# A graph network with dense adjacency tables: where the one-hots of the degrees, the marks for the scatters, the returned rows and the last convolution's loads stand

## The chip, the cores and the metric

The kernel runs on one core of a Trainium2 chip. The metric is the device time of one execution in microseconds; three executions before the change gave 3894.49, 3894.97 and 3899.32, and the median is 3894.97. The engines are called as the profile calls them: PE is the matrix engine (TensorE), PEld its loading of weights, DVE the vector engine, ACT the scalar engine, POOL is GpSimd, SP the queue that issues most DMAs.

## The reference

A matrix x of 3125 nodes by 256 features goes through four graph layers and four feed-forward layers in turn. Each takes a layer norm of x and is added to x. There are 50000 edges (src, dst, edge_weight); dst is sorted. Cut to the parts that matter here:

```python
edge_index = jnp.stack([src, dst])
x = x + L0_gnn(layernorm(x), ...)   # HW = H @ W; segment_sum(edge_weight * HW[dst], src) + b
x = x + L0_ffn(layernorm(x), ...)   # half of the nodes: gelu(sel @ w1 + b1) @ w2 + b2, times a score
x = x + L1_gnn(layernorm(x), ...)   # two convolutions; deg = count of edges per dst, norm = rsqrt(deg)
x = x + L1_ffn(layernorm(x), ...)   # 8 experts, top 2
x = x + L2_gnn(layernorm(x), ...)   # four weighted sums over edges, two projections
x = x + L2_ffn(layernorm(x), ...)   # 8 experts, top 2
x = x + L3_gnn(layernorm(x), ...)   # two convolutions with counts, layer norms and silu
x = x + L3_ffn(layernorm(x), ...)   # 8 experts, top 1 with a capacity
```

All of it is float32. The degree of a node (the number of its edges by dst, plus one) is needed from the second graph layer on.

## The kernel before, in words

**Tables.** The sums over edges are done as dense matrix products. The nodes are padded to 25 tiles of 128, and 3200 by 3200 tables in DRAM hold what the edges add up to: tw the weights, tcn the counts; for the first two tiles of rows a table of pairs, tp, holds both. The edges lie in 391 chunks of 128. DVE compares the edges' cells with each other (L547), so that each cell is written once; then one indirect DMA of POOL for each chunk (L595) scatters 128 cells. 118 chunks go into tp, chunks 118 to 390 into tw (273), chunks 106 to 390 into tcn (285). As dst is sorted, a row tile k of a table is complete once the chunks up to a bound are scattered.

**The first product.** `l0_gnn` computes tw times HW in nine parts, cut over the row tiles k at 3, 6, 9, 12, 15, 18, 21, 23 and 25. Each part goes through seven chunks of columns (4 tiles, the last 1). For each chunk it loads a tile tt of the table, and DVE adds the product to x (L903). The first part (`low_part`) reads tp, separates it into weights and counts and writes both to tw and tcn; the eight others read tw. Each load is ordered behind the scatters that its rows need (`gate`).

**Degrees.** `degrees` is a generator. Each step builds, for 16 chunks of edges, two one-hot tiles on DVE (op, 16 by 128, and ot, 16 by 25, L765), and PE sums their products into a 128 by 25 tile of counts (L772). There are 25 such groups; at the end come the largest count, the inverse root and its row broadcast. `product` takes two steps after each chunk, beginning with the first part.

**Marks.** Scatters that no load needs yet are held back. `weights` and `counts` issue groups of chunks, and a group stands "behind" a mark, an instruction given with `self.pace(...)`. There are 18 marks: the last sum of each of the nine parts (1 to 9), the end of each of the seven chunks of the first FFN (10 to 16), and two places in the start of `l1_gnn` (17, 18). PACE_W gives the chunks of tw at which the groups are cut, PACE_C those of tcn, counted from chunk 106. Chunks of tw below the first number stand behind no mark.

**Loads and memory.** PE's operands are loaded by SP in program order. A load waits until the memory that it writes is free, so the place of a tile in its pool decides which old tile it waits for; everything behind it in SP's queue waits too. Three such places matter:

- The first convolution of `l1_gnn` streams tcn (L256), while SP also loads small tiles of later layers, among them a tile "flat" for a bias (L150), which lies on the memory of the counts and their indices, cnt and idx_c.
- After the second FFN (experts, `tiles`), ACT's queue loads the returned rows of both experts of each node into a ring zt, and DVE adds them to x (L2012). Then `L2_gnn` loads a weight W0 (L143), and `spmm_rows` streams tw (L297).
- Before the last graph layer, SP loads its two weights (L143), the affine parameters gamma and beta (L1349), the condition (L1351), and then streams tcn (L256) for `spmm`.

L265 and L305 are the matrix products of these layers, L893 that of the first. The two lines that step the degrees are

```python
                    for _ in range(2):
                        next(degrees, None)
```

and the marks of the parts are given by

```python
            self.pace(last)
            ...
                for a, z in parts[1:]:
                    self.pace(product(stream, a, z, kb, 24 // kb))
```

Of the kernel before, what the change touches and what calls it, by code (L numbers as in the profile page):

```python
# [10 lines left out]
F32 = mybir.dt.float32  # L11
# [8 lines left out]
P = 128  # L20
# [4 lines left out]
D = 256  # L25
# [3 lines left out]
NC = EC + 1  # L29
# [24 lines left out]
PAIRS = last_chunk(LOW * P) + 1  # L54


PACE_W = (235, 260, 286, 311, 337, 363, NC)
PACE_C = (16, 40, 72, 122, 142, 162, 183, 203, 223, 247, 252, 264)


class Net:
# [681 lines left out]
    def degrees(self, pool):  # L743

        nc = self.nc
        dst_i = pool.tile([P, NC], I32, name="dst_i")
        nc.vector.tensor_copy(dst_i, self.col["dst"])

        def part(name, op, by):
            i = pool.tile([P, NC], I32, name=f"{name}_i")  # L750
            nc.vector.tensor_scalar(i, dst_i, by, None, op0=op)
            t = pool.tile([P, NC], F32, name=name)
            nc.vector.tensor_copy(t, i)
            return t

        dp, dt = part("dst_p", ALU.bitwise_and, P - 1), part("dst_t", ALU.logical_shift_right, 7)
        iota = self.psum()
        nc.vector.tensor_copy(iota[:, :P], self.iota)
        deg = self.psum()[:, :NT]
        for g in self.groups:  # L760
            n, a, b = len(g), g[0], g[-1] + 1
            op = pool.tile([P, 2 * GROUP, P], BF16, tag="op", name=self.name("op"), bufs=2)
            ot = pool.tile([P, 2 * GROUP, NT], BF16, tag="ot", name=self.name("ot"), bufs=2)
            for o, d, m in (op, dp, P), (ot, dt, NT):
                nc.vector.tensor_tensor(  # L765
                    o[:, :n, :],
                    d[:, a:b, None].to_broadcast([P, n, m]),
                    iota[:, None, :m].to_broadcast([P, n, m]),
                    op=ALU.is_equal,
                )  # L770
            for i, c in enumerate(g):
                nc.tensor.matmul(deg, lhsT=op[:, i, :], rhs=ot[:, i, :], start=c == 0, stop=c == NC - 1)  # L772
            yield
        most, all_ = pool.tile([P, 1], F32, name="most"), pool.tile([1, P], F32, name="all")
        nc.vector.tensor_reduce(most, deg, AX.X, ALU.max)
        ps = self.psum()
        nc.tensor.transpose(ps[0:1, :P], most, self.ident)
        nc.vector.tensor_copy(all_, ps[0:1, :P])
        few = pool.tile([1, 1], F32, name="few")
        nc.vector.tensor_reduce(few, all_, AX.X, ALU.max)  # L780
        nc.vector.tensor_scalar(self.few_i, few, 4095.5, None, op0=ALU.is_lt)
        root = pool.tile([P, NT], F32, name="root")
        nc.scalar.activation(root, deg, AF.Sqrt, bias=self.ones[:, 0:1])
        nc.vector.reciprocal(self.dinv, root)
        self.broadcast_row(self.dinv, self.dinv_row)
# [60 lines left out]
    def l0_gnn(self, keep, ordered, clear, fill):  # L846


        nc, ins, x = self.nc, self.ins, self.x
        score = keep.tile([P, NT, 1], F32, name="score")  # L850
        wr, br = keep.tile([P, KD, 1], F32, name="wr0"), keep.tile([1, 1], F32, name="br0")
        nc.sync.dma_start(wr, ins["L0_ffn_wr"].rearrange("(k p) o -> p k o", p=P))
        nc.sync.dma_start(br, ins["L0_ffn_br"].rearrange("(o n) -> o n", o=1))
        with self.reusing("l0g") as pool:
            hw = self.hw
            fm0 = self.nm_tile("fm0").rearrange("p t d -> p (t d)").rearrange("p (k n) -> p k n", k=KD)
            degrees = self.degrees(pool)
            half = len(clear) // 2
            for part in clear[:half]:
                part()  # L860

            def chunk(t0, nt):
                s = slice(t0 * P, (t0 + nt) * P)
                nn = self.normed(pool, t0, nt)
                nc.vector.tensor_add(x[:, t0 : t0 + nt, :], x[:, t0 : t0 + nt, :], nn[:, :nt, :])
                yield
                yield
                yield
                self.to_fm(nn, 0, nt, lambda k, ps: self.copy(k, fm0[:, k, s], ps))
                yield from self.logits_fm(pool, fm0[:, :, s], t0, nt, wr, br, score)  # L870


            rows = self.tw[0:V, :].rearrange("(k p c) o -> p k (c o)", p=P, c=NP)
            steps = iter(())
            kend = KEND[ordered]
            parts = list(zip((0,) + kend, kend))

            def product(stream, a, z, kb, bufs):
                nonlocal steps
                for t0, nt in CHUNKS:  # L880
                    tt = stream.tile([P, kb, 512], F32, tag="tt", name=self.name("tt"), bufs=bufs)
                    tt = tt[:, : z - a, : nt * P]
                    if a or not ordered:
                        ld = nc.sync.dma_start(tt, rows[:, a:z, t0 * P : (t0 + nt) * P])
                        self.gate(ordered, ld, "w", z * P)
                    else:
                        self.low_part(stream, tt, t0, nt)
                    for i0 in range(0, nt, 2):
                        m = min(2, nt - i0)
                        ps = self.psum()[:, : m * D]  # L890
                        for i in range(m):
                            for j in range(a, z):
                                nc.tensor.matmul(  # L893
                                    ps[:, i * D : (i + 1) * D],
                                    lhsT=tt[:, j - a, (i0 + i) * P : (i0 + i + 1) * P],
                                    rhs=hw[:, j, :],
                                    start=j == a,
                                    stop=j == z - 1,
                                )
                                if (j - a) % 3 == 2 or j == z - 1:  # L900
                                    next(steps, None)
                        part = x[:, t0 + i0 : t0 + i0 + m, :].rearrange("p t d -> p (t d)")
                        last = nc.vector.tensor_add(part, part, ps)  # L903
                    for _ in steps:
                        pass
                    for _ in range(2):
                        next(degrees, None)
                    if z == NT:
                        steps = chunk(t0, nt)
                        next(steps)  # L910
                return last

            with self.reusing("low") as stream:
                last = product(stream, *parts[0], parts[0][1], 2)
            for part in clear[half:]:
                part()
            fill()
            self.pace(last)
            with self.reusing("high") as stream:
                kb = max(z - a for a, z in parts)  # L920
                for a, z in parts[1:]:
                    self.pace(product(stream, a, z, kb, 24 // kb))
                for _ in steps:
                    pass
        return fm0, score[:, :, 0]

# [410 lines left out]
    def l3_gnn(self, after, ordered):  # L1337
        nc, ins = self.nc, self.ins
        g = lambda s: ins[f"L3_gnn_{s}"]
        if not ordered:  # L1340
            self.few = self.truth(self.few_i)
        with self.reusing("l3g", side="right") as pool:
            ws = [self.square(pool, f"L3_gnn_W{l}") for l in (1, 2)]
            wide = lambda s: pool.tile([P, D], F32, name=self.name(s))
            aff, cond = [], []
            for l in (1, 2):
                aff.append([wide(s) for s in ("gamma", "beta")])
# [29 lines left out]
            h = pair("h")  # L1377
            bounds = [0, 1, 2, 5, 10, 15, 20, 25]
            for t0, t1 in zip(bounds, bounds[1:]):
# [11 lines left out]
                for i in range(n):  # L1391
                    a = pool.tile([P, 1, D], F32, tag="aff", name=self.name("aff"), bufs=3)
# [6 lines left out]
            h2 = pair("h2")  # L1399
# [23 lines left out]
                yield from after(pool, t0, nt)  # L1423

            def body(dt):
                self.spmm(self.tcn, h, pool, first, dt, 3, lead=2)
                self.spmm(self.tcn, h2, pool, second, dt, 3)

            if ordered:
                body(F32R)  # L1430
# [212 lines left out]
class Experts:  # L1643
# [253 lines left out]
    def tiles(self, pool, side, then):  # L1897
        net, nc, ins, tc = self.net, self.nc, self.ins, self.net.tc
        name, ht, affine, func, summed = self.name, self.ht, self.affine, self.func, self.summed
        rows, z, pars = self.rows, self.z, self.pars  # L1900
        ring = lambda s, shape, n: [pool.tile(shape, F32, name=net.name(s)) for _ in range(n)]
        xbs, pars_, b2s = ring("xb", [P, D + 2], 4), ring("par", [P, self.np_], 4), ring("b2", [P, D], WBUFS)
        ybs, zts = ring("yb", [P, D], 4), [] if summed else ring("zt", [P, 2, 4, D], 4)
        w1s, w2s = zip(*((*ring("w1", [P, KD, ht * P], 1), *ring("w2", [P, ht, D], 1)) for _ in range(WBUFS)))
        why = "counts of experts, at most 7, and truths"

# [174 lines left out]
```

## Time and profile before

| what | us |
|---|---|
| median of three executions | 3894.97 |
| the profiled execution | 3892.81 |
| its span | 3890.8 |
| PE busy | 3484.7 |
| DVE busy | 1324.0 |
| POOL busy | 1060.2 |
| ACT busy | 789.6 |
| one-hots on DVE, op / ot (L765, 25 each) | 55.8 / 13.9 |
| matmuls of the degrees on PE (L772, 391) | 13.9 |
| scatters into tw (L595, 273) | 267.7 |
| scatters into tcn (L595, 285) | 285.6 |

The profiled execution is 2.2 us below the median, and its span, from the first to the last instruction, is 2.0 us below its own time. Times "at" a number of us below are counted from the start of that span. A wait's releaser is what ended it; where several things were waited for, it is the last by the profile.

The stages on that scale: tables to about 350, the first product to 688, the first FFN to 906, the second graph layer from 938 on, returned rows of the second FFN from 1598, the third graph layer from 1642, the fourth from 3234, the last FFN from about 3600.

### The profile page before, as it was taken

What the parts mean: (1) busy time and instruction counts of PE and PEld (TensorE: products, weight loads), DVE (VectorE), ACT (ScalarE), POOL (GpSimd) and SP (SyncE); (2) the same over time, 40 slices, a digit from 0 to 9 for tenths busy, and PEclk for the clock granted to TensorE, in tenths of its full rate; (3) what the DMA queues carried; (4) which work ended last, traced back from release to release, by engine and by line L of the source; (5) the groups of instructions that cost most, each with busy time, mean ns of one, the idle gap of its engine ahead of it and who ended that gap; (6) DMA issues with size and microseconds to landing.
All of it is one profiled execution on the core that took longest, in us unless ns stands there. A gap on an engine that the chain in (4) does not pass through costs nothing. (4 is left out here: it accounts for less than half of the span.)

```text
span 3890.8 us, 45871 instructions
## 1 busy us (share of the span) xinstructions
PE 3484.7 (90%) x16848; PEld 2638.2 (68%) x16848; DVE 1324.0 (34%) x4523; ACT 789.6 (20%) x1748; POOL 1060.2 (27%) x1020
## 2 busy tenths in 40 slices
PE   6775979899799789599999999999899997999698
PEld 4654867557687579488744688644599996877344
DVE  9976214944014553400000000022441116323333
ACT  3320000213012234200000000011244445222222
POOL 5776557777200045100000000000133330000232
PEclk7767989989899899799999999999999998999799
DMA  8789334002677389644444444444344557686441
GB/s 325 285 281 328 102 102 125 1 1 82 213 232 230 121 283 347 200 155 158 152 136 148 139 149 152 150 155 157 120 106 109 171 145 248 219 265 217 101 99 30
DMA packets 430038, 655.67 MB, mean 169 GB/s; under 512 B 62929, under 2 KB 206057, under 8 KB 429804
## 3 DMA queue, kind: packets, MB, share of 16 engines
q1 hardware_dynamic: 366590, 585.97, 45.0%
q0 software_dynamic: 48560, 50.07, 5.8%
q10 hardware_dynamic: 14654, 16.60, 1.3%
q8 instruction: 135, 2.21, 0.2%
q14 instruction: 99, 0.81, 0.1%
HBM read 622.05 MB, written 128.56 MB: 193 GB/s over the span
## 5 line engine op out<-in xcount | busy, mean ns | idle before, releaser
L265 PE MATMUL ps<-tt,h 128*128 128x512 f32 (+1 forms) x2800 | 1074.7, 466 | 52.1 <-DMA tt<-tcn 52.1
L265 PEld LDWEIGHTS ps<-tt,h 128*128 128x128 f32 x2800 | 515.7, 190 | 392.6 <-issue 288.4
L893 PE MATMUL ps<-hw,tt 128*128 128x256 f32 x1250 | 289.1, 392 | 55.2 <-DMA tt<-tw 47.4
L1956 PE MATMUL ps<-xe,w 128*128 128x128 f32 x2688 | 321.5, 276 | 10.5 <-DMA w<-in_L_ffn_W 8.6
L1956 PEld LDWEIGHTS ps<-xe,w 128*128 128x128 f32 x2688 | 317.2, 192 | 18.8 <-issue 11.7
L305 PE MATMUL ps<-n,tt 128*128 128x256 f32 x1250 | 272.2, 381 | 46.4 <-DMA tt<-tw 46.4
L1965 PE MATMUL ps<-w,hid 128*128 128x256 f32 x1344 | 312.7, 383 | 0.0
L595 POOL DMA_INDIRECT tw<-tot,idx_w x273 | 267.7, 980 | 156.3 <-issue 80.4
L595 POOL DMA_INDIRECT tcn<-cnt,idx_c x285 | 285.6, 1002 | 89.7 <-issue 86.2
L893 PEld LDWEIGHTS ps<-hw,tt 128*128 128x128 f32 x1250 | 244.1, 198 | 92.0 <-issue 47.5
L305 PEld LDWEIGHTS ps<-n,tt 128*128 128x128 f32 x1250 | 239.0, 191 | 79.7 <-issue 46.8
L1237 POOL DMA_DIRECT2D L_ffn_z<-x x5 | 3.8, 766 | 1005.6 <-DVE bn L1176 929.6
L305 PE MATMUL ps<-h,tt 128*128 128x256 f32 x1250 | 270.0, 379 | 0.0
L1965 PEld LDWEIGHTS ps<-w,hid 128*128 128x128 f32 x1344 | 248.8, 192 | 29.9
L265 PE MATMUL ps<-tt,lo 128*128 128x512 f32 (+1 forms) x700 | 260.7, 379 | 0.0
L265 PE MATMUL ps<-tt,h_lo 128*128 128x512 f32 (+1 forms) x700 | 259.9, 378 | 0.0
L1959 ACT ACTIVATE hid<-ps,par 128x128 f32<-128x128 f32 x672 | 225.9, 364 | 166.5 <-PE ps L1956 138.6
L305 PEld LDWEIGHTS ps<-h,tt 128*128 128x128 f32 x1250 | 237.5, 190 | 32.3
L1973 POOL DMA_INDIRECT L_ffn_z<-yb,to x112 | 149.1, 1331 | 318.9 <-ACT hid L1959 236.3
L345 PE MATMUL ps<-w,fmc 128*128 128x256 f32 x700 | 173.0, 400 | 17.4 <-ACT fmc L1077 13.8
L1130 DVE TENSOR_SCALAR h<-ps 128x256 f32<-128x256 f32 x24 | 10.2, 425 | 515.8 <-PE ps L305 515.8
L547 DVE SCALAR_TENSOR_TENSOR eq<-cells,dinv_row,ahead 128x256 bf16<-128x256 f32 (+3 forms) x391 | 179.8, 518 | 0.0
(408 smaller groups left out, 3952.1 us busy)
## 6 DMA issues: line engine op xcount, KB each, us to landing
tt<-tw SPq DMA_DIRECT2D x120, 1280.0 KB
tt<-tcn SPq DMA_DIRECT2D x119, 1280.0 KB
w<-in_L_ffn_W SPq DMA_DIRECT2D x112, 1024.0 KB
w<-in_L_ffn_W SPq DMA_DIRECT2D x112, 512.0 KB
tw<-zero_row SPq DMA_DIRECT2D x23, 1600.0 KB
tcn<-zero_row SPq DMA_DIRECT2D x25, 1472.0 KB
tt<-tw SPq DMA_DIRECT2D x36, 768.0 KB
w<-in_L_ffn_w SPq DMA_DIRECT2D x18, 1024.0 KB
```

Source lines behind the costliest of these rows:

```text
L265: nc.tensor.matmul(pair[m], lhsT=part[:, k, m * P : (m + 1) * P], rhs=tt[:, j, :].bitcast(dt), start=k == 0 and i == 0, stop=k == NT - 1 a ...
L305: nc.tensor.matmul(ps[i], lhsT=tt[:, j, i * P : (i + 1) * P], rhs=h[:, k, :], start=k == 0, stop=k == NT - 1)
L345: self.nc.tensor.matmul(ps, lhsT=fm[:, k, i * P : (i + 1) * P], rhs=w[:, k, :], start=k == 0, stop=row is None and k == KD - 1)
L547: nc.vector.scalar_tensor_tensor(eqs[j], cells[k][:, at : at + m], self.col["w"][:, j : j + 1], ahead[:, GROUP * P - m :], op0=ALU.is_equa ...
L595: st = nc.gpsimd.indirect_dma_start(out=table[:, :], out_offset=bass.IndirectOffsetOnAxis(ap=idx[:, c : c + 1], axis=0), in_=src[:, c, :], ...
L893: nc.tensor.matmul(ps[:, i * D : (i + 1) * D], lhsT=tt[:, j - a, (i0 + i) * P : (i0 + i + 1) * P], rhs=hw[:, j, :], start=j == a, stop=j = ...
L1130: nc.vector.tensor_scalar(new[:, t, :], ps, 0.5, None, op0=ALU.mult)
L1237: put(dst[t0 * P : (t0 + full) * P, :].rearrange("(t p) d -> p t d", p=P), src[:, :full, :])
L1956: nc.tensor.matmul(ps, lhsT=w1[:, k, h * P : (h + 1) * P], rhs=xe[:, k, :], start=k == 0, stop=k == KD - 1)
L1959: nc.scalar.activation(hid[:, h, :], ps, func, bias=par[:, h : h + 1])
L1965: nc.tensor.matmul(ps, lhsT=hid[:, h, :], rhs=w2[:, h, :], start=h == 0, stop=h == ht - 1)
L1973: st = nc.gpsimd.indirect_dma_start(out=z[:, :], out_offset=bass.IndirectOffsetOnAxis(ap=self.to[ph][:, 0, j : j + 1], axis=0), in_=yb, in ...
```

## The change

Four edits.

1. `product` takes one step of `degrees` after each chunk instead of two, and none in the first part; those left after the last part are taken then. The one-hots are placed in DVE's order behind the last sum of the chunk (`self.added`), as an order for the scheduler without a semaphore.
2. PACE_W has six numbers instead of seven and begins with 263 instead of 235; PACE_C has thirteen instead of twelve, with other cuts. The 18 marks stay. Behind mark 1 came chunks 235 to 259 of tw, now 263 to 288. The last of tw and the first counts came behind mark 6, now behind mark 5. Behind mark 11 came counts 142 to 161, now 113 to 132; behind mark 18 came counts 264 to 284, now 245 to 284.
3. In `tiles` the ring zt is allocated ahead of xb, par and b2 instead of behind yb.
4. In `l3_gnn` the two weights, gamma, beta, the condition and the streamed tables of both convolutions come from a pool "l3w" on the right side of the memory; the rest stays in "l3g", now on the left side.

```diff
-PACE_W = (235, 260, 286, 311, 337, 363, NC)
-PACE_C = (16, 40, 72, 122, 142, 162, 183, 203, 223, 247, 252, 264)
+PACE_W = (263, 289, 315, 341, 367, NC)
+PACE_C = (2, 28, 45, 62, 93, 113, 133, 153, 173, 194, 205, 229, 245)
...
+        self.added = None
         for g in self.groups:
...
-                nc.vector.tensor_tensor(
+                one = nc.vector.tensor_tensor(
                     o[:, :n, :],
                     d[:, a:b, None].to_broadcast([P, n, m]),
                     iota[:, None, :m].to_broadcast([P, n, m]),
                     op=ALU.is_equal,
                 )
+                if self.added is not None:
+                    self.order(one, self.added, "the products' sums are needed first", sync=False)
...
-                    for _ in range(2):
+                    self.added = last
+                    if a or not ordered:
                         next(degrees, None)
...
-                for _ in steps:
+                for _ in chain(steps, degrees):
                     pass
...
-        with self.reusing("l3g", side="right") as pool:
-            ws = [self.square(pool, f"L3_gnn_W{l}") for l in (1, 2)]
-            wide = lambda s: pool.tile([P, D], F32, name=self.name(s))
+        with self.reusing("l3w", side="right") as held, self.reusing("l3g") as pool:
+            ws = [self.square(held, f"L3_gnn_W{l}") for l in (1, 2)]
+            wide = lambda s: held.tile([P, D], F32, name=self.name(s))
...
-                self.spmm(self.tcn, h, pool, first, dt, 3, lead=2)
-                self.spmm(self.tcn, h2, pool, second, dt, 3)
+                self.spmm(self.tcn, h, held, first, dt, 3, lead=2)
+                self.spmm(self.tcn, h2, held, second, dt, 3)
...
+        zts = [] if summed else ring("zt", [P, 2, 4, D], 4)
         xbs, pars_, b2s = ring("xb", [P, D + 2], 4), ring("par", [P, self.np_], 4), ring("b2", [P, D], WBUFS)
-        ybs, zts = ring("yb", [P, D], 4), [] if summed else ring("zt", [P, 2, 4, D], 4)
+        ybs = ring("yb", [P, D], 4)
```

As the engines' orders are built: in the changed kernel PE, ACT, DVE and POOL issue their instructions in the order of before except in the first product, and in SP's queue the first part's loads of raw pairs stand ahead of the clears of tcn, and the flat load of L150 two loads of tcn later.

## The prediction

> **What bounds the kernel now.** The page's group table comes first, since the chain of waits holds nothing here (four rows at the very end). TensorE (PE) is busy for 90% of the span, and each column "idle before" names what it waits for:
>
> ```profile
> PE 3484.7 (90%) x16848; PEld 2638.2 (68%) x16848; DVE 1324.0 (34%) x4523; ACT 789.6 (20%) x1748; POOL 1060.2 (27%) x1020
> ...
> L265 PE MATMUL ps<-tt,h 128*128 128x512 f32 (+1 forms) x2800 | 1074.7, 466 | 52.1 <-DMA tt<-tcn 52.1
> ...
> L893 PE MATMUL ps<-hw,tt 128*128 128x256 f32 x1250 | 289.1, 392 | 55.2 <-DMA tt<-tw 47.4
> ...
> L305 PE MATMUL ps<-n,tt 128*128 128x256 f32 x1250 | 272.2, 381 | 46.4 <-DMA tt<-tw 46.4
> ```
>
> So the time to be had lies at three starts of table products, each waiting for a load. The table by stretches, cut at the parts of the first product (k rows 3 to 23), comes next: length, PE, its weight loads, VectorE (DVE), ScalarE (ACT), GpSimd (POOL), granted clock, DMA share, GB/s.
>
> ```profile
> 374.00:416.00 42.00, 40.31 (x227) 35.17 (x228) 12.08 (x20) 3.49 (x8) 0.00 (x0) 0.93 0.70 217
> 416.00:448.00 32.00, 31.80 (x148) 27.65 (x146) 8.42 (x13) 0.00 (x0) 24.26 (x25) 1.00 0.11 27
> 448.00:481.00 33.00, 32.17 (x149) 28.37 (x150) 8.51 (x13) 0.00 (x0) 25.20 (x26) 1.00 0.35 125
> 481.00:526.00 45.00, 35.58 (x153) 30.29 (x151) 8.68 (x13) 0.00 (x0) 25.21 (x26) 0.89 0.33 110
> 526.00:574.00 48.00, 34.98 (x150) 30.09 (x150) 8.72 (x14) 0.00 (x0) 25.23 (x26) 0.86 0.30 103
> 574.00:620.00 46.00, 31.98 (x140) 27.92 (x141) 7.95 (x12) 0.00 (x0) 34.69 (x36) 0.85 0.56 175
> ```
>
> 150 matmuls take 32 us in the second part, but 45 and 48 in the fourth and fifth, at a lower clock. The waits there: PE stands for loads of tw, and POOL, which scatters the edges into tw, stands for the sums x of the products: each waits for the other, because a scatter group stands behind the end of a part, and the next part's load stands behind that group.
>
> ```profile
> PE ps L893 <- DMA tt<-tw: 37.5, 4, 14.1
> ```
>
> ```profile
> POOL tw L595 <- DVE x L903: 73.1, 4, 44.9
> POOL tcn L595 <- issue: 43.5, 143, 0.3
> POOL tw L595 <- issue: 41.4, 136, 0.3
> ```
>
> Last, SP's queue at the other two starts. Each wait's end is the issue of the load that PE then waits for:
>
> ```profile
> SPq L150 <- DMA tcn<-cnt,idx_c: 11.7, 1, 11.7
> ```
>
> ```profile
> SPq L143 <- DMA zt<-L_ffn_z: 39.1, 3, 35.9
> ```
>
> ```profile
> 989.50 0.56 SPq L150 DMA_DIRECT2D flat<-in_L_ffn_b  x1
> 990.16 0.53 SPq L256 DMA_DIRECT2D tt<-tcn  x1
> ```
>
> ```profile
> 3221.41 0.33 SPq L1349 DMA_DIRECT2D beta<-in_L_gnn_beta  x1
> 3221.78 0.48 SPq L1351 DMA_DIRECT2D cond<-cond  x1
> 3222.31 4.81 SPq L256 DMA_DIRECT2D tt<-tcn  x3
> ```
>
> PE is idle from 969.8 to 996.71 (26.9), from 1595.3 to 1641.76 (46.4) and from 3211.0 to 3234.40 (23.4).
>
> [...] the clock reads 0.50 in 1625 to 1632, and each restart in the parts costs about 2.4 us more (34.98 busy against 32.6 for 150 matmuls). [...] Here the flat load follows the last count scatter (issued 984.3) by 5.2 us. [...] the DMA share is 1.02 to 1.05 in 270 to 370[...]. [...] the one-hots here, of 2048 elements and iota in PSUM, take 2.28 us.
>
> **1. One-hots out of the first part.** A whole group costs DVE 2.28 + 0.56 us. Before, ten of them run in 339 to 368 with PE standing for them, 2.1 us a time. That looks like 20 us, but it is covered: part 1's first tt lands at 374.50 whatever PE does, since SP issues it behind the low part's raw loads and the clears of tcn, at a DMA share of 1. The bytes ahead of it are the same afterwards, so I leave the start at 374.5 (bounds -3 and +5, the latter where the engines run dry between raw loads that wait for their four buffers). Removed here: nothing. Added: 22 of the 25 groups of up to 16 small matmuls (three ran in part 1 already) now stand between products on a busy PE; with the clock full, 32 of them spanned 0.96 us in part 1 before (around 403) and 15 spanned 0.53, so 0.43 to 0.5 us a group: +9.5 us. DVE has room (8 to 12 busy of 32 to 42 us). The one-hots follow the chunk's last sum and are ready some 3.7 us later, PE's order reaches them after nine matmuls, 3.9 us: even, so 0 to 0.2 us each; I take 0 and hold 5 for the range.
>
> **2. Scatters' marks for tw.** Groups that stand behind a part's end now reach 26 to 28 chunks further: 263 chunks are free of any mark, 289 come behind the low part, 315 behind part 1, and so on. One takes 0.97 + 0.30 = 1.27 us, 26 take 33 us, a part's length. Before, part 4 needed chunk 312, two behind the third mark's group; now it lies in the group one mark earlier. Each part's load has its scatters a part ahead. So 37.5 us of waits go, and three restarts of 2.4: -44.7. With +9.5 of step 1 the first product ends about 35 us earlier; my walk through the parts (37.8, 35.4, 35.4, 38.9, then 32.5 each) gives 608.6 against 642 for the seventh: -33.
>
> **3. Marks for the counts.** This gives most of it back. The cuts of the counts moved back: 172 of them now stand behind the end of the second chunk of the first FFN (mark 11; from count 113 on), before 143 (from 142 on). That mark passed at 797.4 and would now pass at 764. The measured rate behind it was (985.3 - 797.4)/143 = 1.31 us, so the last scatter comes at 764 + 172 x 1.31 = 989, or 983 at 1.275: as late as before (985.3). In between, POOL would stand idle for some 20 us before each of the marks of the ninth to eleventh group. The flat load of the L2 FFN still waits for the last scatter, as its memory held cnt and idx_c. But it stands two tt loads later in SP's queue: block 2 of the L1 product has ten of its 25 k rows loaded ahead of it, 40 matmuls by 0.23 us = 9.2 us that PE does before it stalls. PE arrives 33 us earlier, works 9.2, and stands from about 946 to 995 or 1002. Gain: 9.2 plus (2 to -5), so 4 to 11; I take 8. Of 33 us, 25 become a longer wait.
>
> **4. Returned rows.** The ring zt is placed first in the pool, so that the memory of W0 and of the next tt loads no longer lies under the last zt. SP's W0 waited to 1631.92 for a DVE add of zt at the end of 1595 to 1638; the DMA engines were empty (share 0.03 in 1625 to 1632). Afterwards W0 waits for returned rows to have landed, not to be added: the zt loads are issued by ACT between 1598.8 and 1621.6. I read W0 at about 1614 and the first tt at about 1619, with 8 us to land under competition: PE starts near 1627 instead of 1641.8. The normed tiles are ready from 1612 on and the last at 1638; PE reaches the last k row after 48 us, so DVE doesn't hold it. -14 (bounds -8 and -20). PE has no gap from here to about 2700, so it stays.
>
> **5. The last convolution.** Its weights and streamed tables go to one side, the rest to the other. W1 comes earlier, but the second beta still stands behind a load of x (SP released at 3221.4), the tt loads stand behind it at 3222, and from 3218 to 3234 the DMA share is 1.02: 0 (bounds -4 and +3). The last FFN's weights may load some 10 us earlier; PE there waits for the planning on DVE and POOL (fetch at 3639): 0.
>
> Sum: -8 - 14 = -22 on the profiled execution of 3892.8 us (span 3890.8), so 3871. The median of the runs is 3895.0, 2.2 above it: 3873.
>
> **Rivals.** (a) The early gain survives: if POOL runs ahead so that the last scatter comes 20 us or more earlier (the marks bind less than I read, or the flat load doesn't wait), 33 + 14 = 47 less: 3848. For it: the POOL row "issue" is short; against it: 172 x 1.31 us. (b) Nothing in the first half: the counts end 8 us later, or the one-hots miss their nine matmuls and PE waits; only the returned rows remain, 3881 to 3886; with returned rows gaining 8 or less, no change, 3890. (c) Slower, by one mechanism: the count scatters end late. The first half's end is the last scatter plus 12 us, minus 9. If a scatter next to the FFN's loads cost 1.5 instead of 1.31, or if the mark at the FFN's second chunk didn't move with the product, the last comes at 764 + 258 = 1022 or 797 + 225 = 1022: 37 later, +28 - 14 = +14: 3909. It decides from 1016 on (31 us later, +8). Against it: 143 of them ran at 1.31 beside the same loads. (d) The changed memory doesn't free W0 (another wait takes the place at 1630): 3887, counted as no change or barely faster.
>
> **Chances.** Forecast (3866 to 3880) 0.47; (a) 0.22; (b) and (d) 0.21, half of it within 0.2%; (c) 0.10. What a measurement of this kernel can tell from no change is about 0.2%, 7.8 us: 3887 to 3903. Faster 0.80, same 0.11, slower 0.09. The range leaves out (c) and the far ends of (a): 3845 to 3889.
>
> **What would show it.** Right: PE's row L893 has under 5 us of "tt<-tw"; the first product's last part ends 30 to 35 us earlier; the wait on "tt<-tcn" of L265 grows from 27 to 43 to 50 us near 946 to 1000; the last count scatter lies at 983 to 990; L305's wait falls from 46 to about 32. Wrong: the row of ot (L765) as a releaser of PE in parts 1 to 4; a last scatter before 970 (then (a)) or after 1000 (towards (c)); W0 issued after 1625.

## The result, and the profile after

The changed kernel takes 3879.97 us, the median of 7 executions (3875.00 to 3883.41); before took 3894.97 in 7 executions (3892.18 to 3899.32). The ratio is 0.9959 (95% interval 0.9947 to 0.9970): 15 us less, where 22 were forecast; 3880 is the upper edge of the band that the forecast gave (3866 to 3880). The profiled execution of the changed kernel (3883.41, span 3881.7) is the slowest of its seven, that of before (3892.81) is among its faster ones, so the two traces differ by 9.1 us of span only.

The page's group table of the changed kernel, the rows that answer to those shown of before (a line behind the edits has a number 3 to 5 higher: L893 is L896, L1956 is L1961):

```profile
PE 3485.0 (90%) x16848; PEld 2635.1 (68%) x16848; DVE 1322.6 (34%) x4523; ACT 789.0 (20%) x1748; POOL 1054.0 (27%) x1020
...
L265 PE MATMUL ps<-tt,h 128*128 128x512 f32 (+1 forms) x2800 | 1075.7, 467 | 81.1 <-DMA tt<-tcn 81.1
...
L896 PE MATMUL ps<-hw,tt 128*128 128x256 f32 x1250 | 286.9, 388 | 62.6 <-DMA tt<-tw 52.1
...
L305 PE MATMUL ps<-n,tt 128*128 128x256 f32 x1250 | 272.2, 381 | 33.7 <-DMA tt<-tw 33.7
```

PE's work is the same; the idle time has moved. L265, the product of the second and the fourth graph layer, waits 29.0 us more (27.2 of them in the second: 54.1 for 26.9), the third layer (L305) 12.7 less. The row of the first product reads as if it had got worse, 62.6 for 55.2. It hasn't: all of its 52.1 is one wait ahead of part 1, which ends at 375.20 (before: 374.50). The one-hots that used to lie in that time are gone from it, so the idle time shows. Inside the parts nothing is left of it, as the table by stretches shows for the same stretches as before:

```profile
448.00:481.00 33.00, 33.00 (x237) 28.85 (x236) 25.67 (x26) 0.00 (x0) 22.91 (x25) 1.00 0.49 146
481.00:526.00 45.00, 45.00 (x318) 39.61 (x317) 27.50 (x35) 3.48 (x8) 29.79 (x31) 1.00 0.39 118
526.00:574.00 48.00, 48.00 (x224) 42.27 (x223) 12.87 (x20) 0.00 (x0) 36.61 (x38) 1.00 0.53 147
```

PE is busy in every microsecond and its clock stands at 1.00, where it fell to 0.86 before. GpSimd (POOL) has 36.6 busy of 48, that is 38 scatters at 1.27 us without a break. The product's last matmul starts at 652.4 instead of 687.1: 34.7 us earlier. The waits of GpSimd between 640 and 1000 show what became of them:

```profile
POOL tcn L595 <- DVE junk L1001: 24.5, 1, 24.5
POOL tcn L595 <- DVE junk L997: 20.3, 1, 20.3
POOL tcn L595 <- DVE x L906: 19.9, 1, 19.9
```

Three marks, 64.7 us in which no counts are scattered. So the last scatter is issued at 986.8 (before: 984.3). The rows of the count scatters and of the second layer's last matmuls (first and last start), of before and then of the changed kernel:

```profile
L595 POOL DMA_INDIRECT tcn<-cnt,idx_c x285: 964/971/1924, 610.3 to 984.3; - x143
L265 PE MATMUL ps<-tt,h_lo x700: 271/392/628, 938.8 to 1338.6; 128*128 128x512 f32 x150, 128*128 128x128 f32 x25
```

```profile
L595 POOL DMA_INDIRECT tcn<-cnt,idx_c x285: 962/967/1738, 554.1 to 986.8; - x143
L265 PE MATMUL ps<-tt,h_lo x700: 272/392/629, 905.7 to 1334.5; 128*128 128x512 f32 x150, 128*128 128x128 f32 x25
```

SP's queue in the changed kernel, and PE behind it, look like this:

```profile
992.18 0.56 SPq L150 DMA_DIRECT2D flat<-in_L_ffn_b  x1
992.79 0.58 SPq L150 DMA_DIRECT2D flat<-in_L_ffn_ln_g  x1
993.41 0.42 SPq L150 DMA_DIRECT2D flat<-in_L_ffn_ln_b  x1
993.94 14.02 SPq L256 DMA_DIRECT2D tt<-tcn  x4
```

```profile
PE ps L265 <- DMA tt<-tcn: 54.1, 1, 54.1
```

The flat load follows the last scatter's start by 5.4 us (before: 5.2). The row of a scatter ends after 0.97 us, so 4.4 us lie between that end and the flat load. The profile names the scatters' DMA, not GpSimd's row, as what ended SP's two waits at L150 between 940 and 1000, 62.9 us together (before, between 960 and 1000: 36.4).

PE reaches the second graph layer's product 33.1 us earlier (905.3 for 938.4) and stands from 945.9 to 999.97. When that layer ends (the last matmul of h_lo starts at 1334.5, before 1338.6), 4.1 us of the 34.7 are left. At the third layer SP now has:

```profile
1615.03 1.86 SPq L143 DMA_DIRECT2D w<-in_L_gnn_W  x2
1620.17 29.45 SPq L297 DMA_DIRECT2D tt<-tw  x7
```

W0 is issued 16.9 us earlier than before (1631.92), and PE starts at 1629.6 instead of 1641.8.

### The profile page after: what moved, and what is told of

Same layout as the page of the kernel before. It is cut to its first block, busy times and chain, and to the rows that moved or that the text cites. A ratio compares the mean times of both kernels' runs of the same rounds, so it can differ in the third digit from the quotient of the medians.

```text
span 3881.7 us, 45823 instructions
## 1 busy us (share of the span) xinstructions
PE 3485.0 (90%) x16848; PEld 2635.1 (68%) x16848; DVE 1322.6 (34%) x4523; ACT 789.0 (20%) x1748; POOL 1054.0 (27%) x1020
## 5 line engine op out<-in xcount | busy, mean ns | idle before, releaser
L265 PE MATMUL ps<-tt,h 128*128 128x512 f32 (+1 forms) x2800 | 1075.7, 467 | 81.1 <-DMA tt<-tcn 81.1
L265 PEld LDWEIGHTS ps<-tt,h 128*128 128x128 f32 x2800 | 516.0, 190 | 423.1 <-issue 289.2
L896 PE MATMUL ps<-hw,tt 128*128 128x256 f32 x1250 | 286.9, 388 | 62.6 <-DMA tt<-tw 52.1
L1961 PE MATMUL ps<-xe,w 128*128 128x128 f32 x2688 | 322.2, 277 | 16.5 <-DMA w<-in_L_ffn_W 14.5
L1961 PEld LDWEIGHTS ps<-xe,w 128*128 128x128 f32 x2688 | 317.7, 193 | 25.4 <-issue 16.6
L896 PEld LDWEIGHTS ps<-hw,tt 128*128 128x128 f32 x1250 | 238.5, 194 | 96.0 <-issue 52.4
L305 PE MATMUL ps<-n,tt 128*128 128x256 f32 x1250 | 272.2, 381 | 33.7 <-DMA tt<-tw 33.7
L305 PEld LDWEIGHTS ps<-n,tt 128*128 128x128 f32 x1250 | 239.0, 191 | 66.8 <-DVE n L206 34.1
L305 PE MATMUL ps<-h,tt 128*128 128x256 f32 x1250 | 270.0, 379 | 0.0
L265 PE MATMUL ps<-tt,h_lo 128*128 128x512 f32 (+1 forms) x700 | 261.7, 381 | 0.0
L265 PE MATMUL ps<-tt,lo 128*128 128x512 f32 (+1 forms) x700 | 261.7, 381 | 0.0
L305 PEld LDWEIGHTS ps<-h,tt 128*128 128x128 f32 x1250 | 237.6, 190 | 32.2
```

The source lines that it names most:

```text
L265: nc.tensor.matmul(pair[m], lhsT=part[:, k, m * P : (m + 1) * P], rhs=tt[:, j, :].bitcast(dt), start=k == 0 and i == 0, stop=k == NT - 1 a ...
L305: nc.tensor.matmul(ps[i], lhsT=tt[:, j, i * P : (i + 1) * P], rhs=h[:, k, :], start=k == 0, stop=k == NT - 1)
L896: nc.tensor.matmul(ps[:, i * D : (i + 1) * D], lhsT=tt[:, j - a, (i0 + i) * P : (i0 + i + 1) * P], rhs=hw[:, j, :], start=j == a, stop=j = ...
L1961: nc.tensor.matmul(ps, lhsT=w1[:, k, h * P : (h + 1) * P], rhs=xe[:, k, :], start=k == 0, stop=k == KD - 1)
```

## The experiments

The first theory is that of the prediction: the first product gains some 33 us, the last count scatter takes most of them away, and the returned rows give the rest. Its main rivals are that something other than the last scatter holds the second layer (the loads of the tables, or PE's own rate), and that moving the one-hots is itself what helps.

The chips were not alike, and nine of the twelve runs can't be read without saying so: three chips ran before in 4214, 4215 and 4248 us, with the engines waiting for their own issue through the first 1300 us (PE 63.2 us at the first product's line and 46.8 at L565, in the fourth kernel's profile), and only on the last chip did it take 3898.6 us, near the 3895 of the first measurement. Whether the chip makes the difference, or something else of those hours, no run shows. Below, "the second kind" means those three chips. Ratios are always to before on the same chip, and a gain in us is the ratio's, taken of before's median, where nothing else is said. Runs are numbered in the order in which they follow. Times within a profile below are those of that kernel's own span.

**Each part alone (chip with before at 4214.32).** Four kernels: before with the late one-hots; with the new cuts; with the ring zt first; with the last convolution's pools. Each takes that edit from the change's diff and nothing else.

> Before, with the one-hots alone put behind the first part (old marks, old places). My theory (the one-hots in the first part were covered by the loads of part 1; behind it they only add work to PE, and the end of the counts follows the product): each part from the fourth on still waits for scatters behind the part before it, so its wait stays (some 13 us for parts 5 and 6), and parts 1 to 4 get about 3 us longer each. The product ends some 8 us later than 687, the second chunk of the FFN and with it the last count scatter as well: 3900 to 3905 us, +5 to +10. Rival (the 31.6 us that PE stood for one-hots were a real loss): part 1 starts before 370 and the time falls by 5 to 20.

Measured: 4251.86, ratio 1.0089 (1.0059 to 1.0118), some 38 us slower, where 5 to 10 were expected for the first kind of chip. The sign is that of the theory, but its reason holds in part only. Part 1 starts at 498.21 here, and at 521.02 and 514.05 in the third and fourth kernel, which have the one-hots and marks of before on the same chip. So on this kind of chip the one-hots in the first part were not covered, as the rival has it. But the parts then take 465.1 us instead of 423.7 and 431.9, and the product ends 17 to 19 us later. That is half of the 38; the profiled execution, the fastest of the six, doesn't show where the rest arises.

> Before, with the new cuts of the marks alone. My theory: the four waits for tw (37.5) and the slow clock after them (7) go, so the product ends at about 643; the second chunk of the FFN ends at about 753, 172 counts at 1.31 us stand behind it, the last at 978, and PE goes on some 13 us later with ten k rows more behind it: 6 + 9 us gained, 3880 (3877 to 3884). Then the one-hots of the whole change cost some 9 us. Rival (the product's gain is kept): 45 us less, 3850. Rival (one-hots and marks need each other, as the one-hots on DVE delay the marks): no more than 5 us gained.

Measured: 4207.24, ratio 0.9976 (0.9962 to 0.9991), 10 us faster (the medians differ by 7); 15 were expected on the first kind of chip.

> Before, with the returned rows' ring allocated first alone. My theory: W0 and the first tt are issued some 12 us earlier, PE's wait at the start of the third graph layer falls from 46.4 to about 34, and all of it stays: 3882 (3880 to 3885). Rival (the competition of tt with the last returned rows, or tiles of the experts that now lie elsewhere, give it back): 3890 or more.

Measured: 4200.84, ratio 0.9961 (0.9947 to 0.9976), 16 us faster (10 to 22). PE's waits for the third layer's first load, from the kernel with the rows' ring first and then from the one without it (the last convolution's kernel, next):

```profile
PE ps L305 <- DMA tt<-tw: 34.1, 1, 34.1
```

```profile
PE ps L305 <- DMA tt<-tw: 46.1, 1, 46.1
```

12.0 us of wait gone, on another chip than the first pair's 12.7. The theory holds.

> Before, with the last convolution's loads on their own side alone. My theory: SP issues the tables 10 to 13 us earlier against the loads of x, which land later; PE's start is bound by the DMA engines and by the first normed tile: -2 to +3 us, 3893 to 3898. Rival (the earlier issue starts PE earlier): -8 or more.

Measured: 4217.15, ratio 1.0002 (0.9986 to 1.0019): no change that the timing can tell. The profiles tell more, as this stretch runs alike on all chips. From the start of the third graph layer's product to that of the fourth's it takes 1591.5 to 1594.8 us in the six kernels without the move (before, runs 1, 2, 3, 10 and 11; mean 1592.8) and 1594.6 to 1598.3 in the eight with it (the changed kernel, runs 4 to 9 and 12; mean 1596.2). The move costs some 3 us in the mean; the two ranges overlap by 0.2, and the pair of before and changed kernel shows 1.4.

**Parts of the whole change undone or mended (chip with before at 4215.48).** The one-hots taken back; the counts' cuts earlier:

```diff
-PACE_C = (2, 28, 45, 62, 93, 113, 133, 153, 173, 194, 205, 229, 245)
+PACE_C = (2, 28, 45, 62, 110, 149, 165, 187, 208, 229, 235, 254, 264)
```

and the flat loads with their own memory, alone and with the one-hots taken back:

```diff
-            with pool("pars") as work:
-                l2_ffn.parameters(work)
+            l2_ffn.parameters(part)
```

> The changed kernel, with the one-hots taken back into the first part (two steps a chunk from the first part on). My theory (part 1 waits for its loads whatever PE does in the first part, so the one-hots there were covered, and behind it they cost PE about 9 us): part 1 starts within 3 us of the changed kernel's, the product ends 7 to 10 us earlier, and so do the second chunk of the FFN, the last count scatter and the start of block 2: 7 to 10 us below the changed kernel, 22 to 25 below before where TensorE isn't held up by its own issue. Rival (moving them out made room for the scatters and loads): the same as the changed kernel or 5 us and more slower.

Measured: 4198.36, ratio 0.9950 (0.9933 to 0.9968), 21 us faster.

> The changed kernel, with the counts' cuts at 2, 28, 45, 62, 110, 149, 165, 187, 208, 229, 235, 254, 264, so that GpSimd has no idle time at the marks of the FFN's first two chunks. My theory (the last count scatter sets when block 2 of the second layer's product goes on): GpSimd scatters without a break from 652, the last at about 943 instead of 987; the flat load stands two loads earlier again, so PE stalls from about 939 to 955 instead of 946 to 1000: 36 us below the changed kernel, about 51 below before (ratio 0.987). Rival (the wait is for the tables' loads, or something else of SP's queue): no gain against the changed kernel. Rival (more scatters beside the FFN slow it): the FFN ends 5 us or more later.

Measured: 4213.87, ratio 0.9984 (0.9972 to 0.9995), where 0.987 was expected: a miss. The last scatter came at 1315.4, only 4 us before that of the next kernel (1319.1), which has the changed kernel's cuts.

> The changed kernel, with the second expert layer's parameter loads (flat) given memory of their own, marks as in the changed kernel. My theory (not the scatters themselves but the one flat load behind the last of them, and what is queued behind it on SP, holds PE): the last scatter stays at about 987, yet PE doesn't stall in block 2, since each block's loads need only the counts of its own columns: 54 us of wait and some 3 of slow clock go, 55 to 60 below the changed kernel, 70 to 75 below before (ratio 0.981). Rival (the loads of the next blocks wait for the last counts themselves): the stall moves to block 3 to 6 and 20 us or more of it stay.

Measured: 4239.59, ratio 1.0051 (1.0031 to 1.0071): 0.5% slower than before, where 1.9% less were expected.

> The last kernel, with the one-hots taken back into the first part. My theory: both effects add, as the product's end now reaches the end of the kernel: 7 to 10 us below the last one, about 80 below before (ratio 0.979). Rival (the product's end is hidden again, by the counts' scatters needed for the later blocks): the same as the last one.

Measured: 4213.17, ratio 0.9990 (0.9976 to 1.0004), where 0.979 was expected.

The changed kernel's own repetition was needed to compare these, on a chip with before at 4248.36:

> The changed kernel itself, once more, beside before on the same chip, since the runs so far were on chips on which before takes 4214 us and the engines wait for their own issue until about 1300 us. If the chip is of the first kind (before at 3895): 15 us below before, ratio 0.996. If of the second kind: there the last count scatter doesn't hold PE, the late one-hots cost some 15 us or more, the marks bring 10 and the returned rows 13 to 16: within 0.3% of before, and about 15 us above the same kernel with the old one-hots.

Measured: 4245.42, ratio 0.9991 (0.9968 to 1.0014). So on such chips taking the late one-hots back is worth 0.4% from chip to chip (fifth kernel against this one), and 0.6%, 26 us, on one chip (eighth against seventh). In the last pair part 1 starts 16 us earlier with the late one-hots (533.0 for 549.5), yet the product ends 27 us later (948.4 for 921.5). The early counts gain nothing beyond the intervals, and freeing the flat loads loses. Two things in the traces speak to the last. The flat tiles in the other pool moved the third layer's weights again: in the seventh kernel SP's W0 stands for returned rows and an add of DVE as in before (38.1 and 8.0 us; before 39.1 and 8.1), and the wait of L305 is 44.0 there and 44.9 in the eighth, not 34. Against the fifth kernel, which differs from the eighth by the flat tiles alone, that is 11.3 us more of wait, of 14.8 between the medians. And the second layer didn't go on before the last scatter even with its loads there. The timeline of the eighth kernel at 1274, of engines and queues together, shows it:

```profile
1273.55 0.96 POOL L595 DMA_INDIRECT tcn<-cnt,idx_c  x1 [0.30 <-issue]
1274.01 0.29 PEld L265 LDWEIGHTS ps<-tt,h 128*128 128x128 f32 x1 [2.51 <-issue]
1274.82 0.96 POOL L595 DMA_INDIRECT tcn<-cnt,idx_c  x1 [0.30 <-issue]
1275.41 0.59 PE L265 MATMUL ps<-tt,h 128*128 128x512 f32 x1 [2.21 <-issue]
1276.09 0.97 POOL L595 DMA_INDIRECT tcn<-cnt,idx_c  x1 [0.30 <-issue]
1276.81 0.29 PEld L265 LDWEIGHTS ps<-tt,h_lo 128*128 128x128 f32 x1 [2.51 <-issue]
```

PE gets one instruction every 1.40 us here and waits for nothing that the profile shows. The scatters beside it don't slow it at once: this layer's matmuls followed each other at 0.23 us from 1228.0 to 1249.2 beside the same scatters, as they do in before on the first chip, and slowed down only then: 39 instructions of PE in the 41 us from 1250 on. The last scatter starts at 1291.3; two more matmuls come at the slow rate, and at 1307 the layer goes on at 0.23. So whether the flat load alone holds PE on a chip of the first kind was not settled by a run: no kernel with free flat loads ran there.

One regularity holds in all eleven profiles so far, on both kinds of chip: the time from the last count scatter's start to that of the last h_lo matmul of the second layer. Before 984.3 to 1338.6, 354.3; the changed kernel 347.7 (its block 2 had ten k rows done); runs 1 to 9 in order 355.3, 356.5, 356.0, 354.1, 357.1, 353.8, 357.3, 357.1, 357.8. The layer's product itself takes 385 to 429 us. That speaks for the scatter, but a coincidence can't be excluded by counting, and on the second kind of chip, with the flat loads free, the layer waited for its issue and not for a load. The last three kernels were made for it.

**Earlier scatters, and fewer (chip with before at 3898.6).** The first has the new cuts and the ring zt first, without the late one-hots and the move of the last convolution. The second has the earlier counts' cuts besides. The third is the changed kernel with 112 scatters left out:

```diff
             for c in chunks:
+                if ordered and table is self.tcn and c >= CUT:
+                    done[c] = done[c - 1]
+                    continue
```

> Before with the new marks and the returned rows' ring first, without the late one-hots and without the move of the last convolution's loads. My theory (the late one-hots and the last convolution's move are the two parts that cost): the fastest of the kernels without other edits. Where engines wait for their own issue (before above 4200): 22 to 30 us below before, ratio 0.993 to 0.995; from the end of the fifth layer's experts to the last layer 3 us shorter than in the changed kernel. Where they don't (before at 3895): 25 us below before. Rival (the last convolution's move is worth nothing either way): the same as the kernel that differs by it, 0.995.

Measured: 3866.68 (3861.38 to 3871.74), ratio 0.9923 (0.9907 to 0.9940), 30 us faster than before; expected were 25. The last scatter starts at 977.3 and the layer ends at 1322.2, 344.9 later. Part 1 starts at 374.56, as in before (374.50), though the one-hots are back in front of it; the last matmul of the product starts at 641.9, in the changed kernel at 652.4. From part 1's start that is 267.3 against 277.2: the late one-hots cost PE 9.9 us. The next two kernels agree: 266.8 with the one-hots in front, 276.4 with the late ones.

> The same, with the counts' cuts at 2, 28, 45, 62, 110, 149, 165, 187, 208, 229, 235, 254, 264. My theory: the end of the second graph layer follows the last count scatter by 354 to 358 us, so what counts is how early that is. Where engines wait for their own issue, scatters and PE share the time and the last one comes within 10 us of the kernel above: the same within 0.3%. Where they don't: the last scatter comes at about 935, 35 us below the kernel above. Rival (GpSimd's waits at the marks set the time in both): 20 us or more below the kernel above in both.

Measured: 3834.90 (3831.97 to 3836.62), ratio 0.9840 (0.9824 to 0.9857): 62 us faster than before, and the fastest of the kernels that do the whole work. Its scatters (first and last start), its queue and its wait:

```profile
L595 POOL DMA_INDIRECT tcn<-cnt,idx_c x285: 964/971/2058, 546.9 to 934.7; - x143
```

```profile
940.50 0.56 SPq L150 DMA_DIRECT2D flat<-in_L_ffn_b  x1
941.17 0.53 SPq L256 DMA_DIRECT2D tt<-tcn  x1
```

```profile
PE ps L265 <- DMA tt<-tcn: 21.9, 1, 21.9
```

The last scatter comes at 934.7 (935 was expected), 42.6 us before that of the kernel above, the wait is 21.9 instead of 55.0, and the layer ends at 1288.9 instead of 1322.2: 33.3 us, of which the whole time shows 31.8 (3866.68 against 3834.90). The distance from the last scatter is 354.2 here, as in before, and 344.9 in the kernel above, near the changed kernel's 347.7. In the changed kernel SP issues twelve table loads of the layer ahead of the flat load, and PE stops 40.6 us after the layer's start; in before it issues ten, and PE stops after 31.4. The order of SP's queue from the flat load on is the changed kernel's in the kernel above (three flat loads, then tables from 984.32 on), and that of before here (a table at 941.17 behind the first). So the stop follows the place of the flat load, and 42.6 us of an earlier scatter bring 33.3: the 9.3 between them are, by the author's estimate, the work ahead of the flat load that is lost again (40.6 less 31.4 is 9.2). The FFN's last matmuls start at the same time (857.4 for 857.9); from its first to its last it takes 203.4 us for 202.3 with the added scatters beside it. For the kind of chip on which the engines wait for their own issue no run of this kernel shows what was expected there.

> The changed kernel without the scatters of the last 112 of 285 chunks of counts (left out: these counts stay zero in the table, so the second and fourth graph layer compute with other numbers); loads, products and marks stay. My theory (the last count scatter, and not the loads of the tables or the products before, sets where the second graph layer goes on): the last scatter comes 140 us earlier, the layer's first product starts within 20 us of the changed kernel's start and then takes its own time, so that its end lies about 355 us or less behind its start instead of 420 to 430, some 60 to 80 us below the changed kernel. Rival (the layer is held by its loads or by PE's own rate, and the constant distance from the last scatter is a coincidence): the end of the layer moves by less than 20 us.

Measured: 3828.27 (3823.72 to 3832.37), ratio 0.9823 (0.9806 to 0.9839): by the ratios 53 us below the changed kernel, short of the 60 to 80 that were expected. The last scatter starts at 835.8, and the second layer's product runs without a wait for a load:

```profile
L601 POOL DMA_INDIRECT tcn<-cnt,idx_c x173: 963/967/1729, 549.0 to 835.8; - x173
L268 PE MATMUL ps<-tt,h_lo x700: 271/392/586, 909.8 to 1279.9; 128*128 128x512 f32 x150, 128*128 128x128 f32 x25
```

From first to last 370.1 us, in the changed kernel 428.8 (905.7 to 1334.5). With the end of the scatters out of the way the layer ends 54.6 us earlier, close to the wait of 54.1 (it starts 4.1 later and runs 58.7 shorter). The distance to the last scatter is now 444, so it was no coincidence: on the first kind of chip the late scatter holds the layer, and nothing else held it in this run. The wait of 54.1 us belongs to the scatters, not to the tables' loads or to PE. That the stop follows the place of the flat load speaks for the flat load as the link; whether the table loads behind it would have had to wait for the scatters themselves, no run on the first kind of chip shows.

## Why the prediction was right, step by step

- **One-hots out of the first part**: "Removed here: nothing" holds on the first kind of chip. Part 1 starts at 375.20 in the changed kernel, 374.50 in before, 374.56 with the one-hots back. "+9.5 us" for the matmuls measured 9.9, and PE waits for no one-hot in parts 1 to 4.
- **Marks for tw**: 37.5 us of waits and the slow clock after them are gone, and the product's end moved by 34.7 where "-33" was walked out. The criterion for it was badly put: PE's row was to show under 5 us of "tt<-tw", and shows 52.1, all of it in front of part 1, where before the one-hots filled the time. A restart's 2.4 us is a little low: the prediction's own rows give 32.2 to 32.4 us for 150 matmuls, so 34.98 is 2.6 to 2.8 more; that is 1 us in the sum.
- **Marks for the counts**: the last scatter was to come at 983 to 990, and came at 986.8; PE was to go on at 995 to 1002, and did at 999.97; the wait was to grow to 43 to 50 and grew to 54.1. The 43 to 50 doesn't fit the prediction's own step, which has PE standing from 946 to 995 or 1002, that is 49 to 56; the step was right and the figure drawn from it was not. GpSimd's idle time at three marks, forecast as some 20 us each, was 19.9 to 24.5. The step's term of 8 us measured 4.1 in the pair of profiles, the lower end of its bounds, 4 to 11. 9.2 us of work done ahead less 3.3 us of a later start give 5.9; the other 1.8 are not accounted for.
- **Returned rows**: -14 was the term, 12 to 12.7 the wait measured; W0 was to be issued at 1614 and was at 1615.03. In the pair of profiles only 8.1 of it arrive (1338.6 to 1641.8, 303.2 us; then 295.1), because the second FFN's experts took 221.6 us from their first matmul to that wait in before's profile, and 224.4 to 227.2 in the profiles of all thirteen other kernels, among them the three that keep the ring where it was (225.7 to 226.6). The author takes it for a chance of before's execution, and a good part of why the spans differ by less than the medians. The load may not be the only thing at this start any more: in the sixth and eleventh kernel the profile names DVE's normed tile as what ended the wait of 34, and in the changed kernel PE's weight load waits for that tile equally long (34.1). Whether a still earlier load would gain anything, no run tried.
- **The last convolution**: 0 was the term, about +3 in the means, at the bound that was named, 1.4 in the pair of profiles. SP issues its tables at 3208.85, 13.9 us after the experts' last first-stage matmul (before: 15.0), PE's wait is 24.9 for 23.4. Why, no run shows.

Sum by measured terms: -4 - 12 + 3 = -13, beside -15.0 of the medians. The mechanisms of the two terms that the forecast rests on were right; each came out smaller than forecast. The rival that the early gain survives (3848) was a statement about the marks, not about the hardware: with other cuts and without the late one-hots and the last convolution's move it does survive, in 3834.90.

The change's own parts pull against each other. Late one-hots lose 10 us, the last convolution's move 3, and the counts' cuts throw away some 32 that the tw cuts won. These are figures of the first kind of chip. The cuts behind the FFN's first chunks are the ones to move; the two other parts are to be left out.

## What to carry to other kernels

When one engine's early gain disappears, look for the resource that ends late whatever that engine does, and measure the distance from its last event to the end of the stage in several kernels: a constant distance points to it, and a kernel without those events shows it. How the resource holds the stage can still differ, as on the two kinds of chip here. A limit that holds work back "to keep pace" has to move when the work that it follows moves, otherwise it becomes the bound; its idle time shows on the paced engine (64.7 us of GpSimd's waits for marks here), while the row of the one that waits in the end (PE, 54.1 us) names a load. And idle time on the bounding engine is not a loss where a load ends it anyway: on the first kind of chip the one-hots that PE waited for cost nothing there and 10 us where they were put instead.

## What was not expected of the hardware

The same program took 3895 us in the first measurement and 3899 on the last chip, but 4214 to 4248 on three others. The difference lies in the time up to the last count scatter (1306.7 in the fourth kernel for 984.3 in before, 322 of the 330 us between the spans of these two profiles), where engines wait for their own issue: PE 63.2 us at the first product's line in the fourth kernel (that row has none before), and in the eighth 39 PE instructions in 41 us from 1250 on, one in 1.40 us from 1264 to the last count scatter at 1291.3, in place of a matmul in 0.23. What makes the issue slow there stays open; the profile names no releaser, and no run was made to find it. Its consequence was measured: there the late one-hots cost 38 us with the old marks and 26 with the new ones and the flat loads free, where on the first kind of chip they cost 10 with the new ones, and of the whole change nothing is left that the timing can tell (0.9991, 0.9968 to 1.0014).
